# Relative values of an attention: summed over a query's places on TensorE's column tiles before the output product

## The chip, the cores and the metric

One Trainium2 chip, of which the kernel uses one core. The metric is the time of one execution on the device in microseconds, as the median of several runs. All data is float32.

## The reference

A layer of attention with relative positions, then a layer of routed experts, each between two layer norms and with a residual. x is 16 batches x 512 tokens x 128; there are 16 heads of 8, and relative offsets are cut at 128 on either side.

```python
def attn(x):                     # S = 512, H = 16 heads, hd = 8, M = 128
    q, k, v = (proj(W, b) for W, b in ...)              # b h s d
    idx = clip(r[None, :] - r[:, None], -M, M) + M
    content  = einsum('bhqd,bhkd->bhqk', q, k)
    relative = einsum('bhqd,qkd->bhqk', q, rel_k[idx])
    w = softmax((content + relative) / sqrt(hd))
    out = einsum('bhqk,bhkd->bhqd', w, v) + einsum('bhqk,qkd->bhqd', w, rel_v[idx])
    return out.transpose(0, 2, 1, 3).reshape(B, S, D) @ Wo.T + bo
x = x + layernorm(attn(layernorm(x)))
x = x + layernorm(ffn(layernorm(x)))     # 16 experts, best one of each token, and a shared one
```

The change is in the second einsum of `out`, the relative values, and in the product with `Wo` that follows it.

## The kernel before

The kernel has two stages. In the attention stage (to some 1731 us) a loop of 256 iterations, and 24 more that drain it, works on pieces `(b, c, n)`: batch `b` (16), part `c` (4) and quarter `n` (4). A unit `(b, c)` has 128 queries: 32 from each quarter of the batch. One iteration holds 32 queries of all 16 heads: four score tiles of 128 rows (4 heads x 32 queries) by 512 keys. Everything in this stage is issued through `InOrder` (line 47, which is why nearly all instructions carry L47), so each engine runs the loop body in the order in which it is written. Work of several ages lies side by side in iteration `i`:

- `scores` of piece `i` (PE, tiles `ps`), `peak` (the maxima `nmax`, VectorE) and `exps` (ScalarE, tiles `w`)
- `turn` of piece `i - 1`: transposes of `w` into `pt` on PE, copied to `wT` by VectorE and ScalarE in turn
- `attend` and `attend_near` of piece `i - 5`: weights times values into `pa`, weights times relative values into `pz`
- `output` of the unit that was begun at `i - 9`, in the iterations with `n == 1`, as the `spare` job of that iteration
- in other iterations the `spare` job is a part of the next batch's projections or the turning of the sums (`prt`); the routing of the last batch to experts (`route`) is spread over the iterations as a generator

VectorE is DVE, ScalarE is ACT, GpSimd is POOL; SP issues most DMAs. In `attend` the 128 rows of `pa` are four groups of 32 rows: each product has 32 stationary columns and goes to one column tile, in the order of the groups, for four key tiles. VectorE takes `pa` times the reciprocal sums and a mask (`od`) and adds over the heads (`oT`).

In `attend_near` the stationary operand is a window of `relv`, 4 places x 8 values (32 columns), again on four column tiles. A row of the result `pz` is group `g`, place `j` and value `d`, with four places for four neighbouring queries; only the place that is a query's own counts. With `n == 3` the unit's `pz` is complete: VectorE multiplies it by `Rz`, which holds the reciprocal sum where the place is the query's own and zero elsewhere, and writes `oz` `[128, 4 heads of the group, 128 queries]`.

`output` then forms `py`, queries by features: `oT` times `wo`, and for each of the four `h` the slice `oz[:, h]` times `woz[:, h]`. `woz` holds the rows of Wo four times, once for each place, so that the product sums over places too. Its rows are loaded by 16 DMAs in `later_loads`. `pa`, `py`, `prt` and the products of the projections and of the routing all take turns in one PSUM bank (`bank`, pool `ps_o` with one buffer): the next user's first product waits until the last reader of the one before is done.

The second stage (1731 us to the end) runs the experts on blocks of 128 tokens.

Of the kernel before, what the change touches and what calls it, by code (L numbers as in the profile page):

```python
# [9 lines left out]
F32 = mybir.dt.float32  # L10
I32 = mybir.dt.int32
AF = mybir.ActivationFunctionType
ALU = mybir.AluOpType
AX = mybir.AxisListType
# [3 lines left out]
P = 128  # L18
S = 512
D = 128  # L20
H = 16
HD = 8
# [3 lines left out]
HG = 4  # L26
HH = H // HG
# [23 lines left out]
def relative_attention_then_moe(  # L51
# [6 lines left out]
    nc = tc.nc  # L58
# [35 lines left out]
    with ExitStack() as actx:  # L94
        wp = actx.enter_context(tc.tile_pool(name="attn_w", bufs=1))
        dp = actx.enter_context(tc.tile_pool(name="attn_dram", bufs=1, space=DRAM))
        bp = actx.enter_context(tc.tile_pool(name="attn_batch", bufs=2))
        up = actx.enter_context(tc.tile_pool(name="attn_unit", bufs=2))
# [5 lines left out]
        pe, act, dve, sp_q, pool = (InOrder(tc, e) for e in (nc.tensor, nc.scalar, nc.vector, nc.sync, nc.gpsimd))  # L104
# [52 lines left out]
        vext = dp.tile([LR, HD], F32, name="vext")  # L157
        relv = wp.tile([P, 384, HD], F32, name="relv")

        woz = wp.tile([P, HH, D], F32, name="woz")  # L160

        def relative_keys():
            dve.tensor_copy(rext[:, 0:127], rext[:, 127:128].to_broadcast([HD, 127]))
# [8 lines left out]
        def later_loads():  # L172
            sp_q.dma_start(vext[0:127, :], rel_v[0:1, :].to_broadcast([127, HD]))
            sp_q.dma_start(vext[127 : 127 + NR, :], rel_v)
            sp_q.dma_start(vext[384:LR, :], rel_v[NR - 1 : NR, :].to_broadcast([LR - 384, HD]))
            va = vext[:, :]
            sp_q.dma_start(
                relv.rearrange("p t d -> p (t d)"),
                bass.AP(va.tensor, va.offset, [[HD, P], [1, 384 * HD]]),
            )  # L180
            sp_q.dma_start(wo, WoT)
            wo_v = WoT.rearrange("(g h d) o -> g d h o", g=HG, h=HH)
            for g in range(HG):
                for j in range(4):
                    r = g * 32 + j * HD
                    sp_q.dma_start(woz[r : r + HD, :, :], wo_v[g])
            sp_q.dma_start(bo_r, bo.partition_broadcast(P))
            sp_q.dma_start(wr, w_routerT)

# [13 lines left out]
        nc.gpsimd.memset(mz4, 1.0)  # L203
        nc.gpsimd.affine_select(mz4, mz4, [[-32, HG], [HD, 4]], ALU.is_ge, 0.0, base=-24, channel_multiplier=1)
        nc.gpsimd.affine_select(mz4, mz4, [[32, HG], [-HD, 4]], ALU.is_ge, 0.0, base=24 + HD - 1, channel_multiplier=-1)

        batch, wts = {}, {}

        def bank(shape, name):
            return ps_o.tile(shape, F32, tag="o", name=name)  # L210
# [161 lines left out]
        def exps(b, c, n, g):  # L372

            w = up.tile([P, S], F32, tag="w", name=f"w{b}_{c}_{n}_{g}", bufs=8)
            act.activation(
                w, wts[b, c, n][g], AF.Exp, bias=wts[b, c, n, g], accum_out=wts[b, c][1][:, n, g : g + 1]
            )
            wts[b, c, n, g] = w
# [39 lines left out]

            return leave

        def attend(b, c, n):

            wT = wts[b, c][0]
            v = batch[b]["v"]
            Rh = batch[b, c, "R"][0]
            if n == 0:
                batch[b, c, "oT"] = up.tile([P, NKT * 4, TQ], F32, tag="oT", name=f"oT{b}_{c}")
            oT = batch[b, c, "oT"]
            pa = bank([P, P], f"pa{b}_{c}_{n}")
            for kt in range(NKT):  # L430
                vn = 1 if kt <= n - 2 else 2 if kt >= n + 2 else 0
                for g in range(HG):
                    r = slice(g * 32, (g + 1) * 32)
                    pe.matmul(
                        pa[r, :], v[:, vn, kt, r], wT[:, n, g, (kt - n) % NKT, :],
                        start=(kt == 0), stop=(kt == NKT - 1),
                    )
            t = slice(n * 4, n * 4 + 4)

            def leave():  # L440
                od = up.tile([P, 4, HH, TQ], F32, tag="od", name=f"od{b}_{c}_{n}")
                dve.tensor_mul(od, pa.rearrange("p (t h q) -> p t h q", h=HH, q=TQ), Rh[:, t])
                dve.tensor_reduce(oT[:, t], od.rearrange("p t h q -> p t q h"), AX.X, ALU.add)

            return leave
# [37 lines left out]

        def output(b, c):

            oT, oz = batch.pop((b, c, "oT")), batch.pop((b, c, "oz"))
            if c == 0:
                y_sb[b] = bp.tile([P, NC, D], F32, tag="y", name=f"y_sb{b}")
                mv_y[b] = bp.tile([P, NC, 2], F32, tag="mv_y", name=f"mv_y{b}")
            py = bank([P, D], f"py{b}_{c}")  # L490
            pe.matmul(py, oT.rearrange("p t q -> p (t q)"), wo, start=True, stop=False)
            for h in range(HH):
                pe.matmul(
                    py, oz[:, h].rearrange("p t f q -> p (t f q)"), woz[:, h, :], start=False, stop=(h == HH - 1)
                )

            def leave():
                dve.tensor_add(y_sb[b][:, c, :], py, bo_r)
                stats(sp, mv_y[b][:, c, :], y_sb[b][:, c, :], "ly", dve)

            return leave
# [189 lines left out]
        dve.tensor_reduce(mh4, mh.rearrange("p (g h) -> p h g", h=HH), AX.X, ALU.add)  # L691
        dve.tensor_add(mq, mi[:, 0, :], mi[:, 1, :])
        dve.tensor_reduce(mz, mz4.rearrange("p g q -> p q g"), AX.X, ALU.add)
        for f in (x_turn, queries, keys):
            f(0)()
        queries_turned(0)
# [6 lines left out]
        for i in range(total + 24):  # L703
            b, c, n = at(i)
            k = i % 16
            last = i - 1 if 0 <= i - 1 < total else None
            old = i - 5 if 0 <= i - 5 < total else None
            live = i < total
            nxt = b + 1 if b + 1 < B else None

            spare = None
            if 0 < b < B and k == 6:
                routes[b - 1, 0] = route(b - 1)

            if i == total + 1:
                routes[b - 1, 0] = route(b - 1, 0, NC - 1)
            if i == total + 5:
                routes[b - 1, 1] = route(b - 1, NC - 1, NC)
            if n == 0 and 0 <= i - 4 < total:
                sums(*at(i - 4)[:2])  # L720
                spare = lambda: sums_turn(*at(i - 4)[:2])
            if n == 1 and i >= 9 and i - 9 < total:
                spare = lambda: output(*at(i - 9)[:2])
            if 10 <= i < 30:
                clear_rows((i - 10) * NBLK // 20, (i - 9) * NBLK // 20)
            if nxt is not None:
                if k == 0 and b + 2 < B:
                    load_x(b + 2)
                if k in (6, 7, 14, 15):
                    f = {6: x_turn, 7: queries, 14: keys, 15: values}[k]  # L730
                    spare = lambda: f(nxt)

            if live:
                scores(b, c, n)
            if last is not None:
                T = {g: turn(*at(last), g) for g in ORDER[:2]}
            if live:
                peak(b, c, n, ORDER[0])
                peak(b, c, n, ORDER[1])
                exps(b, c, n, ORDER[0])  # L740
                exps(b, c, n, ORDER[1])
            if last is not None:
                dve.tensor_copy(*T[ORDER[0]])
                act.copy(*T[ORDER[1]])
            if live:
                peak(b, c, n, ORDER[2])
                peak(b, c, n, ORDER[3])
                exps(b, c, n, ORDER[2])
                exps(b, c, n, ORDER[3])
            if old is not None:  # L750
                attend(*at(old))()
                scale = attend_near(*at(old))
            if last is not None:
                dve.tensor_copy(*turn(*at(last), ORDER[2]))
            if old is not None:
                scale()
            if spare is not None:
                leave = spare()
            if last is not None:
                act.copy(*turn(*at(last), ORDER[3]))  # L760
            if spare is not None:
                leave()
            if nxt is not None and k in (0, 2):
                x_stats(nxt, k)
                x_stats(nxt, k + 1)
                if k == 2:
                    x_norm(nxt)

            for r in sorted(routes):


                turns = (n > 0) if nxt is not None else {7: 2, 9: 0, 12: 0, 13: 2, 15: 2}.get(k, 1) if live else 1
                for _ in range(turns):
                    bank_user = next(routes[r], StopIteration)
                    if bank_user is StopIteration:
                        del routes[r]
                        break
                    elif bank_user is not None:
                        bank_user()()
            if n == 1 and i + 3 < total:  # L780
                expand(*at(i + 3)[:2])
# [163 lines left out]
```

## Time and profile before

| | us |
|---|---|
| median of 3 runs | 1997.58 |
| lowest, highest | 1995.7, 1999.06 |
| profiled execution, its time | 1997.39 |
| profiled execution, span of the core | 1995.7 |
| PE busy in the span | 1928.4 |
| DVE busy | 1530.3 |
| ACT busy | 1154.1 |
| POOL busy | 900.1 |

The span runs from the first to the last instruction of the profiled execution. In the rows of groups, `out<-in` names the tiles written and read, then come the form of the TensorE array (rows*columns), the shape, the count, the busy time (overlaps counted once), the mean duration in ns, and the idle time of the engine just before with what ended it. A row of the timeline has start and duration in us, engine, line, operation, tiles and count; instructions that follow each other on an engine and are alike are merged into one row. PE is TensorE's multiplication, PEld its loading of weights. A float32 product counts as two instructions of PE.

### The profile page before, as it was taken

What the parts mean: (1) busy time and instruction counts of PE and PEld (TensorE: products, weight loads), DVE (VectorE), ACT (ScalarE), POOL (GpSimd) and SP (SyncE); (2) the same over time, 40 slices, a digit from 0 to 9 for tenths busy, and PEclk for the clock granted to TensorE, in tenths of its full rate; (3) what the DMA queues carried; (4) which work ended last, traced back from release to release, by engine and by line L of the source; (5) the groups of instructions that cost most, each with busy time, mean ns of one, the idle gap of its engine ahead of it and who ended that gap; (6) DMA issues with size and microseconds to landing.
All of it is one profiled execution on the core that took longest, in us unless ns stands there. A gap on an engine that the chain in (4) does not pass through costs nothing.

```text
span 1995.7 us, 92521 instructions
## 1 busy us (share of the span) xinstructions
PE 1928.4 (97%) x40942; PEld 1545.4 (77%) x40942; DVE 1530.3 (77%) x3857; ACT 1154.1 (58%) x2929; POOL 900.1 (45%) x1004
## 2 busy tenths in 40 slices
PE   6999999999999999999999999999999999779997
PEld 3777777777777777777777777777777777679997
DVE  3677787778787878787877878787878777767776
ACT  3666666666656565656565666666565656334432
POOL 4234353444444453445344434444444534246666
PEclk9999999999999999999999999999999999889999
DMA  2412000000000000000000000000000000065653
GB/s 78 73 24 52 3 22 6 14 13 6 22 5 23 3 25 3 25 3 25 3 24 3 23 4 14 14 6 22 4 18 3 19 5 7 8 177 172 176 162 95
DMA packets 88724, 69.11 MB, mean 35 GB/s; under 512 B 26439, under 2 KB 74724, under 8 KB 88192
## 3 DMA queue, kind: packets, MB, share of 16 engines
q1 hardware_dynamic: 81632, 53.80, 10.2%
q0 software_dynamic: 4384, 8.57, 1.3%
q8 instruction: 321, 5.26, 1.1%
q10 hardware_dynamic: 2304, 0.80, 0.2%
q14 instruction: 83, 0.68, 0.1%
HBM read 44.99 MB, written 18.75 MB: 32 GB/s over the span
## 4 chain that ended last, share of the span: by engine, by line
PE 79%; POOL 8%; DVE 6%; issue 5%; DMA 1%; ACT 1%; SPq 0%; POOLq 0%; ACTq 0%; DVEq 0%
PE ps L47 27%; PE pt L47 24%; PE pa L47 12%; PE pz L47 7%; POOL out_dram L886 4%; PE py L47 4%; DVE nmax L47 3%; POOL lf_rs L80 2%; PE prt L47 2%; POOL f L884 2%; PE pq L47 1%; PE pv L47 1%; PE pl L47 1%; PE pk L47 1%; DVE wT L47 1%
## 5 line engine op out<-in xcount | busy, mean ns | idle before, releaser
L47 ACT ACTIVATE w<-ps,nmax 128x512 f32<-128x512 f32 x1024 | 699.1, 693 | 495.2 <-DVE nmax L47 495.1
L47 DVE TENSOR_REDUCE nmax<-ps 128x1 f32<-128x512 f32 x1024 | 656.1, 683 | 291.0 <-PE ps L47 290.7
L47 PE MATMUL pt<-ident,w 128*128 128x128 f32 x4096 | 590.7, 280 | 3.1 <-DVE wT L47 2.8
L47 PEld LDWEIGHTS pt<-ident,w 128*128 128x128 f32 x4096 | 445.7, 141 | 139.3 <-issue 99.2
L47 ACT COPY wT<-pt 128x512 f32<-128x512 f32 x512 | 299.9, 586 | 153.1 <-PE pt L47 153.0
L47 DVE COPY wT<-pt 128x512 f32<-128x512 f32 x512 | 349.0, 682 | 0.6 <-PE pt L47 0.6
L47 PE MATMUL ps<-kT,qb 32*128 32x288 f32 (+10 forms) x4864 | 326.2, 374 | 5.7 <-POOL qb L47 3.8
L47 PE MATMUL pa<-wT,v 128*32 128x128 f32 x8192 | 276.7, 276 | 2.4 <-ACT R L47 1.2
L47 PE MATMUL ps<-relk,qr 64*32 64x288 f32 (+4 forms) x8192 | 274.8, 377 | 0.0
L47 PEld LDWEIGHTS ps<-kT,qb 32*128 32x128 f32 x4864 | 208.7, 185 | 63.1 <-issue 35.8
L47 PEld LDWEIGHTS pa<-wT,v 128*32 128x32 f32 x8192 | 208.0, 109 | 45.0 <-issue 41.6
L47 POOL TENSOR_TENSOR Rh<-R,mh 128x512 f32<-128x512 f32 x64 | 66.5, 1038 | 357.0 <-ACT R L47 356.9
L47 ACT ACTIVATION_READ_ACCUMULATOR w<-ps,nmax 128x1 f32 x1024 | 212.5, 207 | 0.0
L47 PEld LDWEIGHTS ps<-relk,qr 64*32 64x32 f32 x8192 | 124.3, 106 | 112.1 <-issue 82.0
L47 PE MATMUL pz<-wT,relv 128*32 128x48 f32 (+1 forms) x12288 | 191.4, 210 | 0.2 <-issue 0.2
L47 PEld LDWEIGHTS pz<-wT,relv 128*32 128x32 f32 x12288 | 183.8, 110 | 0.3 <-issue 0.3
L47 POOL TENSOR_TENSOR qr<-qz,mq 128x1024 f32<-128x1024 f32 x64 | 137.5, 2148 | 0.0
L47 POOL TENSOR_SCALAR kT<-kT,kend 128x512 f32<-128x512 f32 x32 | 49.8, 1563 | 150.3 <-ACT sg L47 133.2
L47 DVE TENSOR_REDUCE oT<-od 128x32 f32<-128x128 f32 x256 | 97.4, 381 | 8.9
L849 ACT ACTIVATE x2b<-x2b,xc 128x128 f32<-128x128 f32 x73 | 29.0, 402 | 123.9 <-DVE lf_ve L78 112.8
L47 POOL DMA_INDIRECT rows<-pay,at_i x64 | 68.0, 1062 | 54.8 <-DVE shift L47 44.3
L47 POOL COPY rb<-rt 128x512 f32<-128x512 f32 x64 | 39.0, 609 | 118.0 <-DVE rt L47 108.5
(148 smaller groups left out, 2263.0 us busy)
## 6 DMA issues: line engine op xcount, KB each, us to landing
gu<-_L_ffn_gate_up_proj_dram SPq DMA_DIRECT2D x73, 256.0 KB
dn<-in_L_ffn_down_proj_dram SPq DMA_DIRECT2D x73, 128.0 KB
rows<-zero SPq DMA_DIRECT2D x19, 266.0 KB
xc<-rows SPq DMA_DIRECT2D x8, 532.0 KB
x_sb<-in_L_attn_x_dram SPq DMA_DIRECT2D x64, 64.0 KB
qd<-qp SPq DMA_DIRECT2D x16, 256.0 KB
qz<-qd SPq DMA_DIRECT2D x248, 16.0 KB
relv<-vext SPq DMA_DIRECT2D x1, 1536.0 KB
```

What stands on the lines that cost most here:

```text
L47: return lambda *a, **k: self.tc.keep_in_program_order(op(*a, **k))
L80: root.tensor_tensor(rs, ve, mhalf[:, 0:n], ALU.pow)
L849: nc.scalar.mul(x2[:, 1, :], x2[:, 0, :], x[:, D + 2 : D + 3])
L884: nc.gpsimd.tensor_add(f, f, x[:, 0:D])
L886: own_rows("out", nc.gpsimd.indirect_dma_start(out_rows, bass.IndirectOffsetOnAxis(ap=to, axis=0), f, None, bounds_check=B * S - 1, oob_is ...
```

## The change

A matrix of zeros and ones, `msum` `[128, 32]`, is made at the start: row `32g + 8j + d` has its one in column `8g + d`. In the iteration of `output`, after the products of `attend` into `pa`, four products (`join_places`) take it as stationary operand and `oz[:, h]` as the moving one, for each `h` on its own column tile; they write rows `32h` to `32h + 31` of a second half of `pa`'s tile in the same bank. Row `32h + 8g + d` of the result is value `d` of head `h` of group `g`, summed over the places. VectorE copies it to `oj` ahead of `od`. `output` multiplies `oj` by `wo_h`, the rows of Wo in that order, in one product in place of four. `wo_h` has one copy of Wo's rows and is loaded by 16 smaller DMAs. The last unit, which has no `attend` beside it, takes a bank of its own (`pj`).

```diff
-        woz = wp.tile([P, HH, D], F32, name="woz")
+        wo_h = wp.tile([P, D], F32, name="wo_h")
...
-            wo_v = WoT.rearrange("(g h d) o -> g d h o", g=HG, h=HH)
-            for g in range(HG):
-                for j in range(4):
-                    r = g * 32 + j * HD
-                    sp_q.dma_start(woz[r : r + HD, :, :], wo_v[g])
+            wo_v = WoT.rearrange("(g h d) o -> h g d o", g=HG, h=HH)
+            for h in range(HH):
+                for g in range(HG):
+                    r = h * 32 + g * HD
+                    sp_q.dma_start(wo_h[r : r + HD, :], wo_v[h, g])
...
+        mj = wp.tile([P, 4, HG, HD], F32, name="mj")
+        nc.gpsimd.memset(mj, 1.0)
+        for sign in (1, -1):
+            nc.gpsimd.affine_select(
+                mj, mj, [[-sign * HD, 4], [-sign * 32, HG], [-sign, HD]], ALU.is_ge, 0.0, base=0, channel_multiplier=sign
+            )
+        msum = wp.tile([P, HG, HD], F32, name="msum")
...
-        def attend(b, c, n):
+        def join_places(pj, b, c):
+
+            oz = batch.pop((b, c, "oz"))
+            for h in range(HH):
+                pe.matmul(
+                    pj[h * 32 : (h + 1) * 32, :], msum.rearrange("p g d -> p (g d)"),
+                    oz[:, h].rearrange("p t f q -> p (t f q)"), start=True, stop=True,
+                )
+            oj = up.tile([P, P], F32, tag="oj", name=f"oj{b}_{c}")
+            batch[b, c, "oj"] = oj
+            return lambda: dve.tensor_copy(oj, pj)
+
+        def attend(b, c, n, done=None):
...
-            pa = bank([P, P], f"pa{b}_{c}_{n}")
+            both = bank([P, 2, P], f"pa{b}_{c}_{n}")
+            pa = both[:, 0]
...
+            summed = join_places(both[:, 1], *done) if done is not None else lambda: None
 
             def leave():
+                summed()
                 od = up.tile([P, 4, HH, TQ], F32, tag="od", name=f"od{b}_{c}_{n}")
...
-            oT, oz = batch.pop((b, c, "oT")), batch.pop((b, c, "oz"))
+            oT, oj = batch.pop((b, c, "oT")), batch.pop((b, c, "oj"))
...
             pe.matmul(py, oT.rearrange("p t q -> p (t q)"), wo, start=True, stop=False)
-            for h in range(HH):
-                pe.matmul(
-                    py, oz[:, h].rearrange("p t f q -> p (t f q)"), woz[:, h, :], start=False, stop=(h == HH - 1)
-                )
+            pe.matmul(py, oj, wo_h, start=False, stop=True)
...
+        dve.tensor_reduce(msum, mj.rearrange("p j g d -> p g d j"), AX.X, ALU.add)
...
+            done = at(i - 9)[:2] if n == 1 and 0 <= i - 9 < total else None
...
+            if old is None and done is not None:
+                join_places(bank([P, P], f"pj{b}"), *done)()
             if old is not None:
-                attend(*at(old))()
+                attend(*at(old), done=done)()
                 scale = attend_near(*at(old))
```

## The prediction

> **What bounds the kernel now.** I read the page first (shares, slices, chain), then who TensorE waited for, then the groups of TensorE and VectorE by shape, and last the timeline of one iteration that holds an `output`. The page:
>
> ```profile
> span 1995.7 us, 92521 instructions
> PE 1928.4 (97%) x40942; PEld 1545.4 (77%) x40942; DVE 1530.3 (77%) x3857; ACT 1154.1 (58%) x2929; POOL 900.1 (45%) x1004
> PE   6999999999999999999999999999999999779997
> PE 79%; POOL 8%; DVE 6%; issue 5%; DMA 1%; ACT 1%; SPq 0%; POOLq 0%; ACTq 0%; DVEq 0%
> ```
>
> TensorE (PE) is busy in 97% of the span, and in 9 tenths or more of every slice of the attention stage (85 to 1731 us). The chain that ended last runs 79% through it. That alone would not do, as the share is an average: so the stage itself. In 85 to 1700 us the windows view gives PE 1604.13 busy of 1615.00, at a granted clock of 1.00. The list of PE's waits holds no entry over 10.1 us, and the largest that recurs is `prt` on `od` (7.7 us in 14 times). A nanosecond taken from PE's queue here should be a nanosecond off the time, unless something else is close behind.
>
> The groups that the change touches, and those that I price by:
>
> ```profile
> L47 PE MATMUL pa<-wT,v 128*32 128x128 f32 x8192 | 276.7, 276 | 2.4 <-ACT R L47 1.2 <-DVE od L47 0.8 <-DVE y_sb L47 0.4
> L47 PE MATMUL py<-woz,oz 128*128 128x128 f32 x512 | 67.8, 275 | 0.1
> L47 PE MATMUL py<-wo,oT 128*128 128x128 f32 x128 | 26.3, 287 | 0.3 <-DVE oT L47 0.3
> L47 DVE TENSOR_TENSOR od<-pa,Rh 128x128 f32<-128x128 f32 x256 | 72.0, 281 | 1.4 <-PE pa L47 1.4
> ```
>
> A float32 matmul of the code is two instructions: 64 units x 5 products x 2 = 640 for `py` (512 + 128). Their mean durations (275, 276 ns) overlap in the pipeline, so a price must come from starts. Here is the second half of an iteration with `output`, PE and VectorE (DVE):
>
> ```profile
> 984.36 1.08 PE L47 MATMUL pa<-wT,v 128*32 128x128 f32 x32
> 985.26 0.75 PE L47 MATMUL pz<-wT,relv 128*32 128x64 f32 x48
> 985.94 0.66 PE L47 MATMUL pt<-ident,w 128*128 128x128 f32 x4
> 986.01 0.28 DVE L47 TENSOR_TENSOR od<-pa,Rh 128x128 f32<-128x128 f32 x1
> 986.33 0.38 DVE L47 TENSOR_REDUCE oT<-od 128x32 f32<-128x128 f32 x1
> 986.35 0.30 PEld L47 LDWEIGHTS py<-wo,oT 128*128 128x128 f32 x2
> 986.43 0.41 PE L47 MATMUL py<-wo,oT 128*128 128x128 f32 x2
> 986.63 0.69 DVE L47 COPY wT<-pt 128x512 f32<-128x512 f32 x1
> 986.68 1.06 PE L47 MATMUL py<-woz,oz 128*128 128x128 f32 x8
> 987.57 0.60 PE L47 MATMUL pt<-ident,w 128*128 128x128 f32 x4
> 987.77 0.29 DVE L47 TENSOR_TENSOR y_sb<-py,bo_r 128x128 f32<-128x128 f32 x1 [0.45 <-PE py L47]
> ```
>
> From start to start, `py` holds PE from 986.43 to 987.57: 1.14 us, in which nothing else runs on it. `pa`, on four column tiles, starts its 32 instructions (four rounds of eight) in 985.26 - 984.36 = 0.90 us: 0.225 per round.
>
> **The change part by part.**
>
> *Removed from PE:* the four products with `woz`, eight instructions, 987.57 - 986.68 = 0.89 us, so 0.111 each.
>
> *Added to PE:* the product with `wo_h`, two instructions of that shape, 0.22 us; and four products with `msum`, one per column tile. These have the form of one round of `pa`: 128 rows, 32 columns, 128 moving elements, all four tiles in turn, same bank. So 0.225 us. Net per unit: 0.89 - 0.22 - 0.225 = 0.445 us less on PE. The built order puts the four directly between `pa` and `pz`, and they wait for nothing new of weight: `oz` was made an iteration earlier (at 980.92 for this unit, for a product that would start near 985.3).
>
> *A rule that speaks against it.* The trace shows what a change of array form costs: eight transposes into `pt` from 983.34 to the first `pa` at 984.36 take 1.02 us, where eight products of full form take 8 x 0.111 = 0.89: about 0.13 us more. The Trainium skill, "TensorEngine Tiling (Array Packing)", section "Key Properties", says that changing the tiling mode, not just the tile, drains TensorE. By that rule a little product of 32 columns set into `output`, between two of full form, would pay two switches, 0.26 us, and the gain would be 0.445 - 0.26 = 0.185 us per unit, 11 us in all. But the order shows `pa`, the four, `pz`: all in 128x32 form, the same two switches around them as now. I take no switch.
>
> *Added to DVE:* a copy `oj` of 128x128 from PSUM ahead of `od`. No such copy is in the trace; `od`, of the same size and source, takes 0.281, and `y_sb` 0.292. A copy is not dearer than a product here (copy `wT` of 128x512: 682 ns mean; product `g` of 128x512: 678). Its pitch is at least 0.20 (`od` begins up to 0.08 before the reduction ahead of it ends, by the starts of single instructions) and at most 0.32 (`od` to `oT`, which waits for `od`). I take 0.22, as `oj` and `od` are independent. Is it on the path? The same page, section "PSUM Bottleneck", warns that tiling speeds up TensorE but not the evacuation of PSUM, and here this is near. The one bank of pool `ps_o` passes from `pa` to `py` when `od` has read it: `od` ends at 986.30 and the weights of `py` load at 986.35. By the starts of single instructions this load comes 29 ns after the last transpose (986.32), where loads in such a row come 2 ns after, so `od` releases it already, with the products themselves not yet late. DVE runs without a break from the maxima to `od`, so the copy moves the release by 0.22. But PE arrives later too, by the 0.225 of the join. The two shifts cancel: with 0.20 PE waits for nothing; with 0.32 it waits up to 0.095 us, x 62 = 6 us. I take none, and keep both ends.
>
> *What follows on DVE.* `y_sb` now waits 0.45 us for `py`. DVE will be free 0.22 later and `py` done 0.445 earlier less that shift, so the copy fills idle time. The next maximum waited over 0.6 us in nearly all these iterations (0.79 after this one), and keeps about 0.2 less. ACT's last exponential ends at 986.98; the next scores start at 987.6 at the earliest. So PE is not stopped there. POOL's expansion and the routing keep their order on every queue.
>
> *Start.* `woz` was 16 transfers on SP's queue; `wo_h` is 16 at the same place, each 4 KB instead of 16, so those behind (`bo_r`, `wr`, the next `x`) are not later. On POOL, a fill and two selects of 128x128 are added: 0.20 + 2 x 0.30 by those of `before`. POOL then waits 2.39 us for `lx_ve`; that covers 0.8. Without this cover all of it would delay the first scores. On DVE the reduction to `msum` (0.4 by `oT`) falls in the 8.9 us that DVE idles before the first `v`. Nothing.
>
> *End.* The last unit has no `pa` to share a bank with: its products, copy and bank release stand in a chain, 0.22 + 0.3 (pipeline) + 0.28 + 0.1, while `py` has six instructions less (0.67), part of them waited for: +0.4 us. At the unit whose next maximum has no idle time (1701 us) 0.2 of the gain is lost. The next to last unit is in a stretch of waits: taken as 0.
>
> *Sum.* 62 units x 0.445 = 27.6 saved, less 0.4 and 0.2: 27.0. Of the profiled execution's 1997.39 us (span 1995.7), that leaves 1970.4, a span of 1968.7. The median of the runs, 1997.58, lies 0.2 above that execution: 1970.6. I say 1970.5.
>
> **The rivals.**
> 1. *The bank comes late.* `oj` and `od` together move the release past PE's arrival by 0.1 to 0.3 us per unit. For: the release is 0.05 us ahead of the load, and DVE has no slack in between. Against: the copy's pitch would have to be over 0.3. Then 62 x 0.145 to 0.345 is saved, 9 to 21: 1976 to 1988.
> 2. *PE's time goes back to another wait.* The shorter iteration meets DVE's maxima or ACT's exponentials, which set the pace of the iterations with routing (after 969 us the chain runs through `nmax`, `wT`, `v`, `pay`). For: DVE is at 77%. Against: those stretches begin with DVE idle (2.0 us before `nmax` at 969.70), so nothing is carried into them. All lost: 1997.
> 3. *The four products do not run side by side* (slower). Their weights are one matrix in all four tiles and their moving data a fresh tensor; if each of the eight instructions took a full 0.111 us and the form were switched twice, the join would cost 0.89 + 0.26 = 1.15 in place of 0.225: 1.15 - 0.67 = 0.48 us per unit lost, 30 us, 2027. It turns from gain to loss where the join costs over 0.67 us. Against: 8192 instructions of `pa` run at 0.028 each in exactly this form, with one moving stream per tile.
>
> That the change doesn't do what it says: the built order shows one join per unit, and `py` from ten instructions to four. That part is excluded.
>
> **How the numbers follow.** Forecast (gain 22 to 29 us) 0.84; rival 1 0.09; rival 2 0.03; rival 3 0.04. The range takes the forecast's own, 1968.5 to 1975.5 with the copy's two ends, a run-to-run spread of 1.7 us on either side (runs before: 1995.7 to 1999.06), and the near part of rival 1: 1967 to 1979. A measurement of this kernel can tell about 0.2%, 4 us, from no change: faster 0.93, same 0.03, slower 0.04.
>
> **What would show it.** Right: per unit `py` starts four instructions in about 0.45 us; the first `pz` follows the first `pa` by 1.12 instead of 0.90 us where the join is; PE's waits for `od` before `py` stay under 0.1 us; PE stays at 97%. The wait of `y_sb` for `py` shrinks from 29.8 us to under 10. Wrong: a wait of `py` on DVE `od` or `oj` in the list (rival 1), more idle time before `ps` or `pt` (rival 2), or a join of over 0.5 us (rival 3). A time over 1980 makes the sum wrong.

## The result, and the profile after

The new kernel takes 1977.39 us (median; 1976.51 to 1977.7) where the kernel before takes 1998.32 in the same comparison: a ratio of 0.9896, with an interval of 0.9879 to 0.9913. The gain is 20.9 us, inside the range (1967 to 1979) and smaller than the forecast of 27. The profiled execution spans 1975.7 us where it spanned 1995.7. In a later comparison the same two kernels gave 0.9872 (0.9858 to 0.9887).

The page of the kernel after, its span, busy shares and chain:

```profile
span 1975.7 us, 92844 instructions
PE 1905.7 (96%) x41070; PEld 1518.6 (77%) x41070; DVE 1539.5 (78%) x3922; ACT 1154.3 (58%) x2929; POOL 901.3 (46%) x1007
...
PE 80%; POOL 8%; DVE 6%; issue 5%; ACT 1%; DMA 1%; POOLq 0%; ACTq 0%; DVEq 0%; SPq 0%
```

PE's busy time falls by 22.7 us and the span by 20.0: the gain is PE's, and PE still carries the chain (80%). In the groups of PE by shape (count, busy time, mean in ns, then idle time before and its releaser) the join has exactly the form of `pa`. Its 25.3 us of busy time overlap with its neighbours; from start to start it costs less, as the timeline below shows. The product with `wo` lists 28.9 us where it listed 26.3 for the same 128 instructions:

```profile
L47 PE MATMUL pa<-wT,v 128*32 128x128 f32 x8192 | 276.7, 276 | 2.0 <-ACT R L47 1.2 <-DVE od L47 0.4 <-DVE y_sb L47 0.4
L47 PE MATMUL py<-wo,oT 128*128 128x128 f32 x128 | 28.9, 307 | 0.5 <-DVE oj L47 0.4
L47 PE MATMUL pa<-oz,msum 128*32 128x128 f32 x504 | 25.3, 273 | 0.0
L47 PE MATMUL py<-wo_h,oj 128*128 128x128 f32 x128 | 24.8, 276 | 0.0
```

The timeline of the same iteration that the prediction showed (batch 9, k = 1; k counts a batch's 16 iterations from 0), PE, PEld and DVE alone:

```profile
972.18 1.08 PE L47 MATMUL pa<-wT,v 128*32 128x128 f32 x32
...
973.08 0.40 PE L47 MATMUL pa<-oz,msum 128*32 128x128 f32 x8
...
973.30 0.75 PE L47 MATMUL pz<-wT,relv 128*32 128x64 f32 x48
973.84 0.28 DVE L47 COPY oj<-pa 128x128 f32<-128x128 f32 x1
...
974.03 0.28 DVE L47 TENSOR_TENSOR od<-pa,Rh 128x128 f32<-128x128 f32 x1
...
974.43 0.30 PEld L47 LDWEIGHTS py<-wo,oT 128*128 128x128 f32 x2
974.47 0.45 PE L47 MATMUL py<-wo,oT 128*128 128x128 f32 x2
...
974.67 0.69 DVE L47 COPY wT<-pt 128x512 f32<-128x512 f32 x1
974.76 0.39 PE L47 MATMUL py<-wo_h,oj 128*128 128x128 f32 x2
...
974.98 0.60 PE L47 MATMUL pt<-ident,w 128*128 128x128 f32 x4
975.28 0.28 DVE L47 TENSOR_TENSOR y_sb<-py,bo_r 128x128 f32<-128x128 f32 x1
...
975.61 0.30 PEld L47 LDWEIGHTS pr<-oh,before 128*128 128x128 f32 x2 [0.27 <-DVE y_sb L47]
```

Three readings. From the first `pa` to the first `pz` it is 1.12 us, as forecast: the join costs 0.22. `py` holds PE for 974.98 - 974.47 = 0.51 us, not 0.47. And `y_sb` no longer waits for `py` (the idle time of 0.45 us before it is gone), but begins as DVE ends the copy `wT`; the next user of the bank, `pr`, waits for `y_sb` longer than the 0.18 us before. The list of PEld's waits has it in sum. After:

```profile
PEld pl L47 <- DVE y_sb L47: 3.8, 14, 0.3
PEld pr L47 <- DVE y_sb L47: 3.5, 13, 0.3
```

Before (us in total, times, longest):

```profile
PEld pl L47 <- DVE y_sb L47: 2.6, 14, 0.2
PEld pr L47 <- DVE y_sb L47: 2.4, 13, 0.2
```

In 27 units the wait grew by 2.3 us together, 0.085 each.

To find where the 20 us come from I compared the lengths of the 256 iterations, from the first `ps` of one to that of the next. Only those with an `output` change in the body of the run: on average by -0.41 us in batches 1 to 14 at k = 5 and k = 9, and by -0.33 and -0.32 at k = 1 and k = 13. Over all batches the four sum to -3.4, -6.2, -6.6 and -5.4 us (k = 1, 5, 9, 13). The other iterations sum to +0.2, the start gives +0.3 and the time after the loop +1.1: together -20.0. The k = 1 sum holds an odd iteration of the last batch: it is 0.98 us longer, where its like are 0.41 shorter. That is not the change's doing. From 0.45 us ahead of its start the granted clock of TensorE is half for 3.41 us, which it is not in the same place of the kernel before. Two rows of the windows view, after and before (stretch; its length, busy time and instructions of PE, PEld, DVE, ACT and POOL; granted clock, share of DMA, GB/s):

```profile
1598.20:1601.61 3.41, 3.41 (x35) 2.00 (x42) 1.02 (x8) 0.00 (x0) 3.41 (x4) 0.50 0.00 0
1618.90:1622.30 3.40, 3.40 (x58) 2.31 (x59) 2.02 (x10) 0.21 (x1) 3.40 (x4) 1.00 0.00 0
```

In another execution of the new kernel (`after_again`, below), which has no such stretch there, this iteration is 1.39 us shorter. Of all thirteen traces, six have the stretch in this place, `before_again` among them, and their iteration is 1.2 to 1.5 us longer than its like; the other seven have neither. Without it the two spans would differ by some 21.4 us.

### The profile page after: what moved, and what is told of

Read it like the earlier page. It is cut to its first block, busy times and chain, and to the rows that moved or that the text cites. A ratio compares the mean times of both kernels' runs of the same rounds, so it can differ in the third digit from the quotient of the medians.

```text
span 1975.7 us, 92844 instructions
## 1 busy us (share of the span) xinstructions
PE 1905.7 (96%) x41070; PEld 1518.6 (77%) x41070; DVE 1539.5 (78%) x3922; ACT 1154.3 (58%) x2929; POOL 901.3 (46%) x1007
## 3 DMA queue, kind: packets, MB, share of 16 engines
q1 hardware_dynamic: 81248, 53.60, 10.5%
## 4 chain that ended last, share of the span: by engine, by line
PE 80%; POOL 8%; DVE 6%; issue 5%; ACT 1%; DMA 1%; POOLq 0%; ACTq 0%; DVEq 0%; SPq 0%
PE ps L47 27%; PE pt L47 24%; PE pa L47 13%; PE pz L47 7%; POOL out_dram L912 4%; DVE nmax L47 3%; POOL lf_rs L80 2%; PE prt L47 2%; PE py L47 2%; POOL f L910 2%; PE pq L47 1%; PE pl L47 1%; PE pv L47 1%; PE pk L47 1%; DVE wT L47 1%
```

## The experiments

My theory after the result: the join and the six instructions cost on PE what was forecast, but two effects by way of DVE that I had set to nothing take 0.04 us in every unit (the bank comes late to `py`) and 0.09 us more at k = 1 and 13, where a bank user of the routing waits for `y_sb`. The rivals: the join costs more than its share of starts (or pays for a change of array form); or the removed products were worth less than their starts on PE.

`join_only`, `no_join`, `switch` and `two_ahead` ran on one chip (5), the other experiments on a second (0); on which one the first comparison ran is not known. On both the kernel before takes 2017 to 2020 us, where it took 1998 first, and some iterations are longer whatever the kernel, those with k = 9 among them (see `before_again`). So I read the experiments by the length of single iterations that do not differ between the comparisons (k = 1, 5 and 13), beside the time. Where a span is set against that of before or of the new kernel, that is `before_again` (2016.2) or `after_again` (1990.7), both of chip 0. This table has batch 6, in us, from the starts in each trace; "release to load" is from the end of the last DVE reader of the bank (`od`, `oj` or both in one) to the first load of weights of `py`, and "py" is from its first product to the next transpose, both at k = 5. Where that load follows the transpose ahead of it at once (`switch`, `fused`, `fused_y`) the release was not waited for.

| kernel | k = 1 | k = 5 | k = 13 | release to load | py |
|---|---|---|---|---|---|
| before | 7.57 | 7.14 | 8.05 | 0.054 | 1.139 |
| after | 7.25 | 6.73 | 7.72 | 0.116 | 0.510 |
| before_again | 7.57 | 7.13 | 8.05 | 0.053 | 1.137 |
| after_again | 7.25 | 6.73 | 7.72 | 0.116 | 0.513 |
| join_only | 7.83 | 7.40 | 8.31 | 0.117 | 1.181 |
| no_join | 7.03 | 6.47 | 7.50 | 0.054 | 0.469 |
| switch | 7.53 | 6.95 | 8.01 | 0.323 | 0.447 |
| two_ahead | 7.41 | 6.93 | 7.88 | 0.117 | 0.519 |
| fused | 7.25 | 6.66 | 7.72 | 0.111 | 0.446 |
| swap | 7.25 | 6.73 | 7.72 | 0.118 | 0.513 |
| swap_y | 7.16 | 6.73 | 7.64 | 0.116 | 0.510 |
| one_behind | 8.29 | 6.73 | 8.72 | 0.118 | 0.512 |
| fused_y | 7.10 | 6.66 | 7.57 | 0.111 | 0.447 |

### join_only: the added part alone

```diff
...
-            pe.matmul(py, oj, wo_h, start=False, stop=True)
+            for h in range(HH):
+                pe.matmul(
+                    py, oz[:, h].rearrange("p t f q -> p (t f q)"), woz[:, h, :], start=False, stop=(h == HH - 1)
+                )
```

> Adds the join and the copy to the kernel before and keeps its four products with woz (the joined values are not used). What the new kernel's trace shows of the join: first pa to first pz 1.116 us where it was 0.897, and the first product of py 0.04 late. If the join costs that and no more, +0.26 us per unit x 62 = +16 us, a span near 2012. If copy and release of the bank hide inside PE's own delay, +0.22 x 62 = +13.6, near 2009. If column tiles ran one after another or a change of array form were paid (rival 3 of the prediction), +0.5 to +1.1 per unit, 2025 to 2065.

Measured: 1.0049 of before (1.0033 to 1.0066), a median of 2030.4 where before has 2019.6, and a span 14.3 us over that of `before_again`. In all three columns the iteration is 0.26 us longer than before: 0.22 join and 0.04 in `py` (1.181 for 1.139). At k = 9, one of the iterations that are longer here, it adds only 0.12 us on average. The join has no hidden price, and rival 3 of the prediction is out.

### no_join: the removed part alone

```diff
...
-            pe.matmul(py, oj, wo_h, start=False, stop=True)
+            pe.matmul(py, oz[:, 0].rearrange("p t f q -> p (t f q)"), wo_h, start=False, stop=True)
...
-                attend(*at(old), done=done)()
+                attend(*at(old))()
```

> Takes the join and the copy out of the new kernel: output multiplies oT by wo and oz[:, 0] by wo_h, so the relative values of three of the four heads of each group are left out. Only the removal of three products is left. If PE's time is the whole price, six instructions x 0.111 = 0.67 us per unit x 62 = -41.5 us against before, a span near 1954. If, as I now think, y_sb is held by DVE in this iteration (it waited 0.45 us for py before and can come only that much earlier), the bank user that follows it in half of the units (pr or pl of the routing) keeps 0.2 us of the 0.67: some 29 x 0.22 = 6.5 us less, near 1961.

Measured: 0.9786 of before (0.9769 to 0.9802). At k = 5 it gives 0.67 us (7.135 - 6.468), which is the six instructions at 0.111; at k = 1 and 13 only 0.54. So 0.13 us of what PE saves is kept by the bank user behind `y_sb` there, less than the 0.22 that I expected, but in the place expected. The total, a span 42.8 us under that of `before_again`, is nearer to the expectation's first number, because other iterations moved too (-8.0 us at k = 6, +10.5 at k = 11); the single iterations decide.

### switch: the join between products of full form

```diff
...
-                T = {g: turn(*at(last), g) for g in ORDER[:2]}
+                T = {ORDER[0]: turn(*at(last), ORDER[0])}
+            both, summed = None, lambda: None
+            if old is not None and done is not None:
+                both = bank([P, 2, P], f"pab{i}")
+                summed = join_places(both[:, 1], *done)
+            if last is not None:
+                T[ORDER[1]] = turn(*at(last), ORDER[1])
...
```

> The new kernel with the four join products issued between the two turns (transposes of full form) that stand ahead of pa, in place of between pa and pz; the copy stays where it is on DVE. Same work, two more changes of array form. If a change of form costs what the starts around pa and pz show (pt to pa 203 ns in place of 109; first pt after pz 165 in place of 109 and 137 ahead of it), some 0.18 us per unit x 62 = 11 us: a span of 1986 to 1987. By the 0.26 that the prediction worked with, 16 us: 1992. If form does not matter, 1976 as the new kernel.

Measured: 0.9907 of before (0.989 to 0.9923), a span of 2000.0, which is 9.3 over that of `after_again`. Its timeline of PE:

```profile
691.99 0.66 PE L47 MATMUL pt<-ident,w 128*128 128x128 f32 x4
692.58 0.43 PE L47 MATMUL pab<-oz,msum 128*32 128x128 f32 x8
692.93 0.66 PE L47 MATMUL pt<-ident,w 128*128 128x128 f32 x4
693.52 1.08 PE L47 MATMUL pab<-wT,v 128*32 128x128 f32 x32
```

From the first transpose to the first product of `pa` it is 1.53 us here, and 1.02 in the new kernel, which has only the eight transposes there. Less the join's own 0.22, two more changes of form cost 0.29 us. At k = 1 and 13 the iteration is longer by that; at k = 5 by 0.22 us and not 0.29, as PE now comes to `py` later than the bank does (`py` 0.447), which gives back 0.07. The section "Key Properties" of the Trainium skill's "TensorEngine Tiling (Array Packing)", which the prediction cites, says that a change of tiling mode drains TensorE, and gives no price; here two changes show as 0.29 us. The price falls on the small product only where that is put among full ones, and `join_places` is not.

### two_ahead: one more copy ahead of the release

```diff
-            return lambda: dve.tensor_copy(oj, pj)
+            ok = up.tile([P, P], F32, tag="ok", name=f"ok{b}_{c}")
+
+            def leave():
+                dve.tensor_copy(ok, pj)
+                dve.tensor_copy(oj, pj)
+
+            return leave
```

> The new kernel with a second copy of the joined values (to a tile nobody reads) ahead of oj and od on DVE. If the release of the bank by DVE is the edge that PE's py now sits on, each further 0.197 us of DVE ahead of od makes PE wait 0.15 to 0.2 us per unit: +9 to +12 us over the new kernel, 1985 to 1988. If DVE had slack there and the copy cost nothing, 1976 to 1977.

Measured: 0.9933 of before (0.9917 to 0.995), a span 17.8 us over that of `after_again`. At k = 5, +0.20 us: the copy's whole pitch; at k = 1 and 13, +0.16. (Over all batches the four iterations with `output` add 8.5 us, as k = 9 adds almost nothing here; another 7 us lie at k = 6, one of the iterations that are longer in these comparisons.) The timeline shows the wait that the new kernel only touches:

```profile
699.53 0.28 DVE L47 COPY oj<-pa 128x128 f32<-128x128 f32 x1
699.73 0.28 DVE L47 TENSOR_TENSOR od<-pa,Rh 128x128 f32<-128x128 f32 x1
...
700.13 0.30 PEld L47 LDWEIGHTS py<-wo,oT 128*128 128x128 f32 x2 [0.24 <-PE pt L47]
700.16 0.46 PE L47 MATMUL py<-wo,oT 128*128 128x128 f32 x2
```

The load of `py` has an idle time ahead of it, and comes 0.117 us after the end of `od`. The label names `pt` as releaser, which was long done; the constant distance to `od` in this kernel and in the new one says that DVE's release set it. DVE has no slack ahead of the bank's release. The trace also shows where the 0.117 us go: a semaphore instruction of its own, which waits for DVE, runs from 0.040 to 0.091 us after the end of `od`, and the load, which itself waits for PE, starts 0.026 later. That instruction is there in the new kernel, in `join_only` and in `two_ahead`. In the kernel before, in `no_join` and in `fused` the load waits for DVE itself, without such an instruction.

### fused: one DVE product for oj and od

```diff
...
-                summed()
-                od = up.tile([P, 4, HH, TQ], F32, tag="od", name=f"od{b}_{c}_{n}")
-                dve.tensor_mul(od, pa.rearrange("p (t h q) -> p t h q", h=HH, q=TQ), Rh[:, t])
+                if key is not None:
+                    odj = up.tile([P, 2, P], F32, tag="odj", name=f"odj{b}_{c}")
+                    dve.tensor_mul(
+                        odj.rearrange("p f k -> p (f k)"), both.rearrange("p f k -> p (f k)"),
+                        Rf[:, 0:8].rearrange("p t h q -> p (t h q)"),
+                    )
...
```

> The new kernel with oj and od made by one DVE product of 128x256 (both halves of the bank times a row of ones followed by Rh; POOL fills the ones, 128x128 per unit). One reader releases the bank, and py waits for DVE alone, where in the new kernel it waits for DVE and for PE in two instructions. oz's product of the same size takes 0.41 us in the trace, so the release comes 0.07 us earlier than by oj and od (0.197 + 0.281). If the late release (0.04 us per unit) and the delayed y_sb (0.09 us in the units with pr or pl) are what the new kernel loses against the sum, it gains 62 x 0.04 + 28 x 0.07 = 4 to 5 us over it: a span near 1971. If the loss has another cause, no change: 1975 to 1976.

Measured: 0.9865 of before (0.9848 to 0.9882). At k = 5 it gains 0.07 us over the new kernel, as forecast: the load of `py` follows the last transpose at once and `py` takes 0.446, four instructions at 0.111. At k = 1 and 13 it gains nothing, against the expectation. PEld's waits for `y_sb` grow to 4.7 (`pl`) and 4.4 (`pr`), so the 0.07 that PE gains there is waited away. Nor can a gain be told in the time: a median of 1991.3 beside 1992.1 for the new kernel on that chip, and at k = 9 the iteration is 0.12 longer on average.

### swap: od ahead of oj

```diff
-                summed()
                 od = up.tile([P, 4, HH, TQ], F32, tag="od", name=f"od{b}_{c}_{n}")
                 dve.tensor_mul(od, pa.rearrange("p (t h q) -> p t h q", h=HH, q=TQ), Rh[:, t])
+                summed()
```

> The new kernel with od ahead of oj on DVE. The bank is released at the same moment, but oT, which waits for od, no longer stands idle for it, and y_sb comes 0.12 us earlier. If the delayed y_sb is what costs 0.09 us in the units with pr or pl (k = 1 and 13), some 28 x 0.09 = 2.5 us less: a span near 1973. If those units lose by the bank's release before py alone, no change: 1975.7.

Measured: 0.9879 of before (0.9863 to 0.9895), each column equal to the new kernel. A miss: `oT` does come 0.12 us earlier, but the copy `wT` behind it waits 0.07 us for the third turn's transposes and starts when it did. So it is not the order of `oj` and `od` that makes `y_sb` late. `y_sb` stands behind a copy of 0.69 us that PE itself releases, and that the join moves back by its own 0.22.

### swap_y: y_sb ahead of that copy

```diff
...
-                dve.tensor_copy(*turn(*at(last), ORDER[2]))
+                third = turn(*at(last), ORDER[2])
+                if n != 1:
+                    dve.tensor_copy(*third)
...
             if spare is not None:
                 leave()
+            if last is not None and n == 1:
+                dve.tensor_copy(*third)
```

> As swap, and in iterations with output y_sb and its statistics are put ahead of the third copy wT on DVE. y_sb then waits for py alone. If y_sb's lateness is the loss, the units with pr or pl gain as in swap and no more than 1 us on top, 1972 to 1973; if the later wT or the later next maximum comes onto the path, it loses: over 1976.

Measured: 0.9865 of before (0.985 to 0.988). At k = 1 and 13 it gains 0.08 to 0.09 us and at k = 5 nothing. PEld's waits for `y_sb` are those of the kernel before again:

```profile
PEld pl L47 <- DVE y_sb L47: 2.6, 14, 0.2
PEld pr L47 <- DVE y_sb L47: 2.4, 13, 0.2
```

That is the whole difference between k = 5 and k = 1: 0.41 against 0.32 us gained by the new kernel. In time, a median of 1991.2 beside 1992.1 does not settle it; the expected 1972 to 1973 in the terms of the first comparison would be 2.7 to 3.7 us, and the span is 2.0 us shorter.

### one_behind: DVE later, but after the release

```diff
                 dve.tensor_reduce(oT[:, t], od.rearrange("p t h q -> p t q h"), AX.X, ALU.add)
+                if done is not None:
+                    ok = up.tile([P, P], F32, tag="ok", name=f"ok{b}_{c}")
+                    dve.tensor_mul(ok, Rh[:, t].rearrange("p t h q -> p (t h q)"), ident)
```

> The new kernel with an additional DVE product of 128x128 from SBUF behind oT in the iterations with a join (its output is read by nobody): DVE gets 0.2 us more per unit, but after the bank is released. If only the units with pr or pl feel it, through y_sb, 28 x 0.2 = 5.6 us: a span near 1981. If all feel it, 62 x 0.2 = 12: 1988. If DVE's lateness is of no account behind the release, 1976.

Measured: 1.0109 of before (1.0094 to 1.0124), so it lost all the gain and more. The size was wrong: the added product did not take the 0.28 us of its like but a median of 1.11. The timeline shows what ran beside it:

```profile
759.70 2.15 POOL L47 TENSOR_TENSOR qr<-qz,mq 128x1024 f32<-128x1024 f32 x1
...
760.89 1.11 DVE L47 TENSOR_TENSOR ok<-Rh,ident 128x128 f32<-128x128 f32 x1
...
762.53 0.27 DVE L47 TENSOR_TENSOR y_sb<-py,bo_r 128x128 f32<-128x128 f32 x1
...
762.86 0.97 PEld L47 LDWEIGHTS pl<-wr,x2T 128*128 128x128 f32 x8 [1.26 <-DVE y_sb L47]
```

It reads two tensors from SBUF, and ends 0.15 us after POOL's `qr`. The Trainium skill, "SBUF — State Buffer", section "Who interferes with whom", states that a VectorE instruction with two SBUF inputs contends with a GpSimd instruction that reads SBUF; the trace agrees. The question is answered all the same, and more sharply: at k = 5 DVE is some 0.9 us later behind the release, and the iteration is not longer (6.73); at k = 1 and 13 it is 1.0 longer, through `y_sb` and the bank. Two other iterations lengthened too. At k = 14 it is 1.5 us in eight of the batches and nothing in the others, and in just these eight the granted clock is half for 3.41 us; batch 6:

```profile
764.56:767.97 3.41, 3.41 (x43) 1.30 (x36) 1.29 (x2) 0.64 (x2) 0.00 (x0) 0.50 0.03 5
```

PE had stood idle for 1.03 us ahead of `pl` there, but it did so in the other batches as well. So 12 us of the loss are the clock's, and the expectation had no term for it. The 0.4 to 0.5 us at k = 10 are not explained.

### before_again, after_again and fused_y, on one chip

`before_again` and `after_again` are the two kernels unchanged; `fused_y` joins the edits of `fused` and `swap_y`.

> The kernel before, unchanged, with a profile on the chip that the other experiments ran on: its runs there are 1% longer (some 2019 us) than those shown first. The traces of the experiments lengthen three iterations of every batch (those after k = 5, 8 and 10) by 0.1 to 0.5 us against the new kernel's first trace, whatever their edit, so I expect the same here: some 1 + 6 + 8 us more in these three and no difference in the iterations with k = 1 and 5. If it is not the chip but what the edits have in common, this trace shows none of it.

> The new kernel, unchanged, on the same chip as the experiments. Ratio to before as first measured, 0.9896 (0.9879 to 0.9913), if the chip's delays hold both alike. If the chip's delays are spent partly in the same stretches that the saved time shortens, the ratio is nearer 0.987, as swap (which in the quiet iterations equals the new kernel to 0.00 us) gave 0.9879.

> fused and the y_sb part of swap_y together: one DVE product for oj and od, and y_sb ahead of the third wT copy in iterations with output. By the two traces, 0.06 us less in the units with k = 5 and 9 (31 of them) and 0.09 or more in those with k = 1 and 13 (29): 4 to 6 us less than the new kernel on the same chip, a ratio of 0.997 to 0.998 between them. If the wT copy that comes later then holds the next transposes, nothing.

Measured: `before_again` 1.0005 of before (0.9997 to 1.0014), with a span of 2016.2. Against the first trace it lengthens by 9.1 us at k = 6, 5.8 at k = 9 and 2.4 at k = 10, and by -1.3 at k = 11: so the edits are not the reason, though the sizes are not those that I gave. That it is the chip is not shown either, as the chip of the first comparison is not known, and the two chips of the experiments agree in it. k = 1, 5 and 13 are equal but for the last batch. `after_again`: 0.9872 (0.9858 to 0.9887). Against `before_again` its four `output` iterations gain 6.2, 6.3, 8.3 and 5.3 us (1.3 of the first are the half clock of `before_again`); of the delays it loses 6.4 us less at k = 6 and 11.1 more at k = 11. In `before_again` the first maximum of k = 6 starts 0.70 us later than in the first trace, though the last score product starts no later, and at k = 9 the products of `pz` pause for 0.5 us. Why, I have not found, and the part of its 25.6 us of span that is theirs cannot be told from the change. The two ratios, 0.9896 and 0.9872, have intervals that overlap.

`fused_y`: 0.9856 (0.9843 to 0.9869), and a median of 1988.5 beside 1992.1 for the new kernel in the same comparison. The intervals overlap, so the times alone do not settle it; in the traces it is 0.07 us shorter at k = 5 and 0.15 at k = 1 and 13, but 0.10 longer at k = 9, and its span is 3.3 us shorter, though it has the half clock in the last batch (1.3 us) and `after_again` has not. The expectation was 4 to 6. At k = 1, 5 and 13 it is the best of the correct kernels run; whether it is faster as a whole is not shown.

## Why the prediction was right, and where its sum was off

- *PE bounds the stage, and what is taken from its queue comes off the time.* Right. At k = 5 `no_join` takes all of 0.67 us from the iteration, and `join_only` adds all of 0.26. At k = 1 and 13 a part is waited away (below).
- *The join costs a round of `pa`, 0.225 us.* Right: 0.22.
- *No change of form is paid.* Right: 0.29 us for two changes shows in `switch`, and in the new kernel nothing of it.
- *The copy's pitch and the release.* The pitch was right (0.197 from `oj` to `od`), and so was the finding that DVE is the edge. "I take none" was a mis-sized term: `py` was to become 0.669 us shorter by six instructions and became 0.629 shorter (1.139 to 0.510), 0.04 us less. That is inside the bound of 6 us that was kept. PE's and DVE's shifts do cancel, but the load came 0.116 us after the release where it came 0.054 before. With a second product and a second reader in the bank, `py` waits for DVE and for PE, in two instructions, where it waited for DVE alone. Where the wait binds, the distance is 0.117 with this form (`two_ahead`) and 0.054 without (`no_join`). The sign that was named for this, a wait of `py` on `oj` in PE's list, could not show it: the shortest wait in these lists is 0.2 us, and the one that is there (0.4, once) is not the 0.04 of every unit.
- *"The copy fills idle time."* This step failed. The idle time of `y_sb` was no free cover at k = 1 and 13: the routing's `pr` or `pl` takes the bank after `py`, and waits for `y_sb`. I had followed DVE's next maximum and not the next user of the bank. Its own figures did not give a cover either: 0.45 us of idle time, less 0.22 that DVE is later, less 0.445 that `py` is earlier, is -0.215. The text took "that shift" off 0.445 once more, where the join's delay of PE is in it already. DVE in fact begins `y_sb` 0.08 before the copy ahead of it ends, and `py` is 0.04 late, which leaves some 0.09. The step costs 0.41 - 0.325 = 0.085 us in 27 units, 2.3 us; `swap_y` recovers it. (The named sign, a wait of `y_sb` for `py` under 10 us, came true at 1.3, but it says only that `y_sb` now waits for the copy.)
- *The end and the rest.* Forecast +0.6 in all. The half clock at the last batch's k = 1 took 1.4 us, which is no part of the change; the time after the loop 1.1, the start 0.3, and the other iterations 0.2 to 0.4. These smaller ones are not explained.

The working: 62 x 0.445 = 27.6 was forecast for the iterations. The late bank, a little offset by a join of 0.219 in place of 0.225, makes 0.41 of 0.445: less 2.2. The late `y_sb`: less 2.3. The half clock: less 1.4. The rest: less some 1.7. That leaves 20, and 20.0 was measured in the spans. None of the three rivals happened; the first was near, in its mechanism and at an eighth to two fifths of its size (0.04 us for 0.1 to 0.3).

## What to carry to other kernels

On an engine that bounds a stage, price instructions by their start-to-start distance in the same form; that term came out to the hundredth here. Then, for each engine that the edit delays, follow every user of what it releases: an engine's idle time is free only up to the next wait on it, and where a pool has one buffer, the tile that takes it next waits too, though it reads nothing of what is written there now. A small product on column tiles belongs next to others of its form. And where one iteration of many is odd, compare the granted clock of that stretch before it is called chance or an effect of the change.

## What the runs showed of the hardware

- A change between products of 128x128 and 128x32 form cost 0.29 us for the way there and back (`switch`).
- Eight instructions on four column tiles (0.22 us) took as long as two of full form (2 x 0.111).
- A load of PE that waits for two engines started 0.117 us after DVE's release, where one that waits for DVE alone started after 0.054. A semaphore instruction of 0.051 us stands between in the first case.
- A DVE product of 128x128 with two SBUF operands took 1.11 us (median) beside a POOL product that reads SBUF, where `od`, with one operand in PSUM, takes 0.28.
- A stretch of 3.41 us at a granted clock of 0.50 made an iteration 1.2 to 1.5 us longer (six traces, the last batch's k = 1; `one_behind`, k = 14). It came in some executions and batches and not in others with the same idle time of PE ahead; the cause stays open.
- The same kernel ran 1% apart in two comparisons (1998 and 2017 to 2020 us) at granted clocks of 0.99, by delays in three or four iterations of each batch.
